# Signs of an adjacency matrix taken in SBUF, and turned by transposing DMAs in place of TensorE

## The chip, the cores and the metric

The kernel runs on one core of a Trainium2 chip. The core has five engines with a queue of instructions each, worked off in order: PE (TensorE, matrix products; its weight loads are shown apart as PEld), DVE (VectorE), ACT (ScalarE), POOL (GpSimd) and SP (SyncE, which here does nothing but issue DMAs). They meet through semaphores. The metric is the device time of one execution in microseconds, the median of several runs; lower is better.

## The reference

It is one layer of a graph network on 16 batches of 1024 nodes with 64 channels. Each node drops some neighbours by their rank in its row of the adjacency matrix, takes three quantiles per channel over what is left, and puts the sum through two small dense layers:

```python
neigh = (adj_ > 0) & ~eye
ni = neigh.astype(jnp.int32)
rank = jnp.cumsum(ni, axis=-1) - ni
nb = ni.sum(-1)
skip = jnp.where(nb > T, (nb + K - 1) // K, 1)          # T, K = 10, 2
skip = jnp.maximum(skip, 1)
sk = skip[:, :, None]
rem = neigh & (sk > 1) & (rank % sk == sk - 1) & mask[:, :, None]
rem = rem | jnp.swapaxes(rem, 1, 2)
adj_d = jnp.where(rem, 0.0, adj_)
nd = adj_d > 0
vals = jnp.where(nd[..., None], x[:, None, :, :], jnp.inf)
s = jnp.sort(vals, axis=2)
...
agg = agg + jnp.asarray(w, x.dtype) * (v_lo + frac * (v_hi - v_lo))   # tau 0.25, 0.5, 0.75
...
out = (1.0 + EPS_GIN) * x + agg
h = jax.nn.relu(out @ W1 + b1)
y = h @ W2 + b2
```

Ahead of it stands a layer norm with a relu (`h`), behind it a residual. The adjacency is symmetric, holds ones and zeros in float32, has ones on the diagonal, and a node has about nine neighbours.

## The kernel before

All of it is `list_layer`; the function `dense_layer` behind a flag doesn't run on this data. A batch goes through a line of generators:

- `load(b)` (L1007): for each of eight tiles of 128 rows, `ask` (L892) has SP fetch 512 KB of adjacency into a buffer `at` (three of them). PE turns it: the upper two bytes of each float are taken as bfloat16 (a view with a step of two), and eight products with the identity (L1021) write two PSUM tiles `tp` of 128x512. A ninth product (L1027) adds a large negative number on the diagonal. Two ACT instructions (L1034) take the sign, once per PSUM tile, into the 8-bit tensor `ne`, which holds the turned matrix as [128, 8, 1024]. There are two buffers `ne`. Batch 0 has every second sign taken by DVE.
- `number(b)` counts the neighbours of each node from `ne` (products `cp`, ACT's `cnt`, L1063).
- `drop(b)` ranks them (products `rk`, ACT's `dist`, L1106, two per row tile) and marks those to drop (`rem`, DVE).
- `keep(b)` combines both directions (products `kp`, ACT's `kept`, L1130) and packs bits (`pack<-code`, L1138).
- `order(b)` and `collect(b)` sort the nodes by degree and write lists of neighbours, `idx`: from `pack<-num` (L1147) through products `codeP` (L1201) and their evacuations `st` and `own` (L1214 to L1219) to the last `idx` (L1253). `choose(b)` fetches the first eight slots of the tile with most neighbours by products (`got`).

The lists then feed gathers: one indirect DMA (L1408) per slot, issued by POOL, brings 128 rows of 64 floats into tiles `g`. The gathers of a pair of batches are sorted along the slots by DVE with minimum and maximum (L1551, L1556), weighted by ACT (L1571), summed by PE (`acc`, L1577) and put through the dense layers. While one pair is sorted, the next one is prepared.

What sets the order on each engine is `arrange`: it gives every instruction a cost (`Step.cost`), schedules the whole program forward and backward some rounds, and fixes each engine's sequence by its best round. The order is thus static; a DMA that lands later than its cost says keeps an engine waiting at that place. Which instruction waits for which data stays with the framework's semaphores. Two buffers' rules matter here: `at` has three buffers, so tile t+3 isn't fetched before tile t is read, and `ne` has two, so batch b+1 isn't written before `keep(b-1)` has read its own.

Of the kernel before, what the change touches and what calls it, by code (L numbers as in the profile page):

```python
# [40 lines left out]
OP = mybir.AluOpType  # L41
# [27 lines left out]
EARLY, AHEAD = 8, 20  # L69
FINAL = (8,4,4,4,0,0,0,0)  # L70
MANY = 10

FEW = 32
GROUP = 8
# [540 lines left out]
class Step:  # L615

    def __init__(self, ins, place):
        self.ins, self.place, self.kind = ins, place, type(ins).__name__
        self.engine = NAMES[str(ins.engine).split(".")[-1]]
        self.reads, self.writes = (  # L620
            [Use(a.bass_ap) for a in aps if getattr(a, "bass_ap", None) is not None] for aps in (ins.ins, ins.outs)
        )
        self.moves = self.kind == "InstDMACopy"
        self.before, self.behind, self.after, self.tail = set(), set(), [], []
        self.busy, self.lag = self.cost()
        self.load = self.lag - 1900

    def cost(self):
# [26 lines left out]
        if self.engine == "POOL":  # L655
            return (1345, 1400) if self.moves else (300 if most <= 128 else 4100, 100)
        by = self.writes[0].size * self.writes[0].count * (self.writes[0].lines[1] - self.writes[0].lines[0])
        return 480, 1900 + by / 390


def spread(steps, waits, ranks, place):
# [169 lines left out]
def list_layer(  # L831
# [106 lines left out]
    nc.vector.tensor_copy(mask.rearrange("p b t -> p (b t)"), mp)  # L938
    below = cst.tile([P, P], BF16, name="below")
    nc.vector.tensor_scalar(below, minus16, MOST, None, OP.mult)  # L940
    near = cst.tile([P, 1], F32, name="near")
    nc.vector.memset(near, -LEAST_EDGE)
    parts = cst.tile([P, NT, P], BF16, name="parts")
# [62 lines left out]

    def load(b, fast=False):  # L1007

        ne = wk.tile([P, NT, N], FP8, name="ne", bufs=2)
        neT[b] = ne  # L1010
        nbs[b] = [wk.tile([P, NT], F32, name=n) for n in ("bias", "half")]
        for t in range(NT):
            ask(b, t)
            at = asked.pop((b, t)).bitcast(BF16).rearrange("p (n two) -> p n two", two=2)[:, :, 1]
            ask(*divmod(b * NT + t + 2, NT))
            for n in range(2):
                tp = psum.tile([P, 4, P], F32, name="tp", tag="mx" if b else "agg", bufs=3 if b else 2)
                run = []
                for s in range(4):
                    m = 4 * n + s  # L1020
                    run.append(nc.tensor.matmul(  # L1021
                        tp[:, s], at[:, m * P:(m + 1) * P], ident16, start=(s == 0), stop=(s == 3 and t // 4 != n),
                        skip_group_check=True,
                    ))
                if t // 4 == n:
                    run.append(
                        nc.tensor.matmul(tp[:, t % 4], below, ident16, start=False, stop=True, skip_group_check=True)  # L1027
                    )
                settle(run)
                to = ne[:, 4 * n:4 * n + 4, t * P:(t + 1) * P]  # L1030
                if not b and n:
                    nc.vector.tensor_scalar(to, tp, 0.0, 0.5, OP.is_gt, OP.subtract, saturate=False)
                else:
                    nc.scalar.activation(to, tp, AF.Sign, bias=near, scale=UP, saturate=False)  # L1034
            if fast and t % 4 == 3:
                number(b, t - 3, t + 1)
            yield 0.1
        if not fast:
            number(b, 0, NT)
        yield 1.4  # L1040

    def number(b, lo, hi):
# [4 lines left out]
        for at in range(lo, hi, step):  # L1047
            cols = slice(at * P, (at + step) * P)

            cp = psum.tile([P, step * P], F32, name="cp", tag="mx", bufs=3)  # L1050
            run = []
            for k in range(2):
                for q in range(4):
                    ones = one if b or q < 2 else twice[:, P:]
                    run.append(nc.tensor.matmul(
                        cp[32 * q:32 * q + 32], ones[:, 1 - k:33 - k], ne[:, 2 * q + k, cols], start=(k == 0),
                        stop=(k == 1), skip_group_check=True,
                    ))
            settle(run)
            if b == 0 and at >= 4:  # L1060
                nc.vector.tensor_scalar(cnt[:, cols], cp, float(P), None, OP.add)
            else:
                nc.scalar.activation(cnt[:, cols], cp, AF.Copy, bias=float(P))  # L1063
# [16 lines left out]
    def drop(b):  # L1080
# [5 lines left out]
        for t in range(NT):  # L1086
            ts = slice(t * P, (t + 1) * P)
            dist = wk.tile([P, N], F16, name="dist")
            for n in range(2):
# [4 lines left out]
                )]  # L1094
                for s in range(4):
                    run.append(nc.tensor.matmul(  # L1096
                        rk[:, s * P:(s + 1) * P], ne[:, 4 * n + s, ts], twice[:, :P] if not b and n else upper,
                        start=False, stop=(s == 3),
                        skip_group_check=True,
                    ))  # L1100
# [9 lines left out]
    def keep(b):  # L1110

        ne, rem = neT.pop(b), rems.pop(b)
        for t in range(NT):
            ts = slice(t * P, (t + 1) * P)
            kept = wk.tile([P, NT, P], FP8, name="kept")
            for n in range(2):
                kp = psum.tile([P, 4, P], F32, name="kp", tag="mx" if b or n else "agg", bufs=3 if b or n else 2)
                side = bool(b <= 3 and n or not b and t % 2)
                run = [] if side else [nc.tensor.matmul(kp, plus, ne[:, 4 * n:4 * n + 4, ts], start=True, stop=False)]
                run.append(nc.tensor.matmul(kp, minus, rem[:, 4 * n:4 * n + 4, ts], start=side, stop=False))  # L1120
                for s in range(4):
                    at = (4 * n + s) * P
# [1 line left out]
                settle(run)  # L1124
                if side:
                    nc.vector.scalar_tensor_tensor(
                        kept[:, 4 * n:4 * n + 4], kp, -1.0, ne[:, 4 * n:4 * n + 4, ts], OP.mult, OP.is_lt, saturate=False
                    )
                else:
                    nc.scalar.activation(kept[:, 4 * n:4 * n + 4], kp, AF.Relu, saturate=False)  # L1130
# [1066 lines left out]
```

## Time and profile before

| | us |
|---|---|
| median of 3 runs | 1337.45 |
| lowest, highest | 1331.23, 1339.11 |
| the profiled execution, its time | 1339.05 |
| the profiled execution, its span (first to last instruction) | 1337.2 |
| mean granted TensorE clock in it | 0.938 |
| DMA: mean rate over the span | 95 GB/s |

The profile is of one execution. "Busy" is the time in which an engine executes something; register, branch, semaphore and DMA-issuing instructions don't count, so SP has no busy time. A group of instructions is a line of the kernel with its engine, operation and shapes: the sum of busy time, the mean of one, then the idle time just before them and what ended it. In a row of windows each engine has its busy time and, in brackets, its number of instructions; PEclk is the granted clock and DMA the mean share of the 16 DMA engines. In the timeline each row has its start, its length, the engine, and in square brackets the idle time before it with the event that came last before the start.

### The profile page before, as it was taken

The numbers are of one execution on the slowest core, as the hardware profiler recorded it, in microseconds if no ns is written. First come the engines' busy times: TensorE is split into PE (matmuls) and PEld (weight loads), VectorE is DVE, ScalarE is ACT, GpSimd is POOL, SyncE is SP. The second block draws the span as 40 slices with busy tenths as digits, with TensorE's granted clock in tenths as the row PEclk, the third lists the DMA queues.
The fourth block names the chain that finished last, engine by engine and source line by source line (L and its number), as shares of the span: only waits on it lengthen the run. The fifth ranks groups of instructions, "written<-read, shape, count | busy, mean of one in ns | idle before, by whom it ended". The sixth has DMA issues, their size and how long they took to land.

```text
span 1337.2 us, 32000 instructions
## 1 busy us (share of the span) xinstructions
PE 1133.7 (85%) x9889; PEld 758.7 (57%) x9931; DVE 1154.8 (86%) x5327; ACT 1101.0 (82%) x3470; POOL 949.3 (71%) x895
## 2 busy tenths in 40 slices
PE   6877789797899998988898899888999999777267
PEld 4555566666556665656565665656566557553144
DVE  6828998859998699965699999999699999999984
ACT  5685899797989997899759995899969998389564
POOL 0177677777777777777777777777777777777740
PEclk9888999998989998999999999999999999787679
DMA  6272526252526251535335252724343122111111
GB/s 230 63 246 54 152 57 171 63 154 55 147 41 187 56 171 33 145 99 146 68 79 151 47 153 56 186 48 131 76 105 90 31 53 60 30 32 42 22 30 29
DMA packets 158739, 126.59 MB, mean 95 GB/s; under 512 B 127163, under 2 KB 127710, under 8 KB 158558
## 3 DMA queue, kind: packets, MB, share of 16 engines
q1 hardware_dynamic: 130078, 95.25, 24.8%
q0 software_dynamic: 28480, 29.20, 11.3%
q8 instruction: 80, 1.31, 0.4%
q14 instruction: 101, 0.83, 0.2%
HBM read 105.62 MB, written 9.05 MB: 86 GB/s over the span
## 4 chain that ended last, share of the span: by engine, by line
ACT 34%; PE 27%; DVE 18%; issue 16%; DMA 4%; POOL 0%; SPq 0%; DVEq 0%; POOLq 0%; ACTq 0%
ACT g L1571 7%; ACT dist L1106 7%; ACT ne L1034 6%; PE codeP L1201 4%; ACT kept L1130 4%; DVE g L1551 4%; DVE g L1556 4%; PE got L1451 3%; PE acc L1577 3%; PE high L1708 2%; DMA g<-gtab,idx 2%; PE kp L1123 1%; DVE keys L1210 1%; DVE found L1241 1%; PE kp L1120 1%
## 5 line engine op out<-in xcount | busy, mean ns | idle before, releaser
L1408 POOL DMA_INDIRECT g<-gtab,idx x856 | 909.7, 1063 | 330.4 <-DMA g<-gtab,idx 132.6
L1551 DVE TENSOR_TENSOR g<-g 128x768 f32<-128x768 f32 (+5 forms) x479 | 290.7, 617 | 15.1 <-PE acc L1631 10.7
L1556 DVE TENSOR_TENSOR g<-g 128x768 f32<-128x768 f32 (+5 forms) x479 | 290.0, 618 | 11.9 <-DMA gg<-g 11.7
L1571 ACT ACTIVATE g<-g,coef 128x64 f32<-128x64 f32 x896 | 254.1, 393 | 36.0 <-DVE g L1551 25.6
L1034 ACT ACTIVATE ne<-tp,near 128x512 fp8e4<-128x512 f32 x248 | 167.7, 763 | 21.8 <-PE tp L1027 12.9
L1577 PE MATMUL acc<-g,kf 128*128 128x128 f32 (+4 forms) x528 | 138.6, 387 | 51.6 <-ACT g L1571 49.9
L1201 PE MATMUL codeP<-pack,perm 128*128 128x332 bf16 x1024 | 171.5, 314 | 6.2 <-DVE perm L1176 6.1
L1106 ACT ACTIVATE dist<-rk,bias 128x512 f16<-128x512 f32 x256 | 170.6, 755 | 4.6 <-PE rk L1096 2.6
L1130 ACT ACTIVATE kept<-kp 128x512 fp8e4<-128x512 f32 x220 | 142.0, 682 | 2.1 <-PE code L1133 1.5
L1201 PEld LDWEIGHTS <-perm 128*128 128x128 bf16 x1024 | 95.6, 100 | 74.3 <-DVE perm L1176 20.6
L1577 PEld LDWEIGHTS acc<-g,kf 128*128 128x128 f32 x528 | 82.5, 200 | 78.4 <-ACT g L1571 68.2
L1021 PE MATMUL tp<-kb,at 128*128 128x128 bf16 x976 | 98.5, 224 | 32.9 <-ACT dist L1106 15.3
L1096 PEld LDWEIGHTS <-ne 128*128 128x128 fp8e4 x1024 | 80.8, 99 | 59.6 <-issue 25.1
L877 DVE MEMSET pause<- 128x1 bf16 x1838 | 108.4, 59 | 0.0
L1096 PE MATMUL rk<-kw,ne 128*128 128x128 fp8e5 x992 | 102.4, 223 | 1.9 <-issue 1.1
L1021 PEld LDWEIGHTS <-at 128*128 128x128 bf16 x976 | 73.2, 101 | 54.0 <-issue 29.1
L1123 PE MATMUL kp<-kw,rem 128*128 128x128 fp8e5 x1024 | 102.0, 218 | 0.0
L1091 PE MATMUL rk<-parts,cnt 128*128 128x512 bf16 x232 | 89.4, 385 | 12.4 <-ACT dist L1106 5.3
L1120 PE MATMUL kp<-rem,kw 128*128 128x512 bf16 x256 | 96.6, 378 | 0.3 <-DVE pause L877 0.3
L1451 PE MATMUL got<-pack,hot 128*128 128x192 bf16 x896 | 96.3, 252 | 0.5 <-DVE y L1762 0.4
L1123 PEld LDWEIGHTS <-rem 128*128 128x128 bf16 x1024 | 73.6, 97 | 38.8 <-issue 0.4
L1107 DVE TENSOR_SCALAR rem<-dist,half 128x1024 bf16<-128x1024 f16 x128 | 63.7, 504 | 24.6 <-ACT dist L1106 20.8
(221 smaller groups left out, 2409.0 us busy)
## 6 DMA issues: line engine op xcount, KB each, us to landing
at<-in_adj_dram SPq DMA_DIRECT2D x122, 512.0 KB
g<-gtab,idx POOLq DMA_INDIRECT x856
xt<-in_x_dram SPq DMA_DIRECT2D x16, 256.0 KB
y<-in_x_dram SPq DMA_DIRECT2D x16, 256.0 KB
gtab<-xt SPq DMA_DIRECT2D x16, 256.0 KB
out_dram<-y SPq DMA_DIRECT2D x14, 256.0 KB
spare<-in_adj_dram SPq DMA_DIRECT2D x6, 512.0 KB
g<-stage SPq DMA_DIRECT2D x14, 160.0 KB
```

The costliest lines, as they stand in the source:

```text
L1021: run.append(nc.tensor.matmul(tp[:, s], at[:, m * P:(m + 1) * P], ident16, start=(s == 0), stop=(s == 3 and t // 4 != n), skip_group_check ...
L1034: nc.scalar.activation(to, tp, AF.Sign, bias=near, scale=UP, saturate=False)
L1096: run.append(nc.tensor.matmul(rk[:, s * P:(s + 1) * P], ne[:, 4 * n + s, ts], twice[:, :P] if not b and n else upper, start=False, stop=(s ...
L1106: nc.scalar.activation(to, rk, AF.Abs, bias=bias[:, t:t + 1])
L1123: run.append(nc.tensor.matmul(kp[:, s], rem[:, t, at:at + P], minus, start=False, stop=(s == 3)))
L1130: nc.scalar.activation(kept[:, 4 * n:4 * n + 4], kp, AF.Relu, saturate=False)
L1201: run.append(nc.tensor.matmul(flat, perm[:, t, k * P:(k + 1) * P], pack[:, t], start=False, stop=(t == NT - 1), skip_group_check=True,))
L1408: ins = nc.gpsimd.indirect_dma_start(out=gathered[m, tiles][:, slot, k - lo, h], out_offset=None, in_=tables[2 * m + h][0], in_offset=bass ...
L1551: nc.vector.tensor_tensor(at(f + k * df, df, many), pa, pb, OP.min if what == "<" else OP.max)
L1556: nc.vector.tensor_tensor(pa if back else pb, pa, pb, OP.max if what == "<" else OP.min)
L1571: nc.scalar.activation(v[:, i, j], v[:, i, j], AF.Copy, scale=w[:, i, j:j + 1])
L1577: nc.tensor.matmul(acc, ident32, lines[:, s], start=False, stop=(s == now[-1] and not ends), skip_group_check=True)
```

## The change

For batches 1 to 15 (`TURN = 1`) PE no longer turns the adjacency. One ACT instruction takes the sign of the whole 128x1024 tile in SBUF and writes it as 8-bit numbers into the first 1024 bytes of each row of the same buffer, so that columns n and n + 512 lie side by side. SP then issues a DMA with a transpose that takes such a pair as one 16-bit number and writes [128, 4, 128] of them into `ne`, so `ne` is now four blocks of pairs, and its readers take it with a step of two bytes. The diagonal, which the ninth product put right, is set by one DVE minimum per batch with `away` (-1 on the diagonal, 1 elsewhere) over the eight diagonal blocks. Batch 0 is turned by PE as before, into the new layout. The planner counts the transposing DMA as a move and gives it a rate of its own.

```diff
+TURN = 1
...
-        self.moves = self.kind == "InstDMACopy"
+        self.moves = self.kind in ("InstDMACopy", "InstDmaTransposeAnt")
...
-        return 480, 1900 + by / 390
+        return 480, 1900 + by / (180 if self.kind == "InstDmaTransposeAnt" else 390)
...
+    away = cst.tile([P, P], BF16, name="away")
+    nc.vector.tensor_scalar(away, minus16, 2.0, 1.0, OP.mult, OP.add)
...
-        ne = wk.tile([P, NT, N], FP8, name="ne", bufs=2)
+        pairs_of = wk.tile([P, NT // 2, N], BF16, name="ne", bufs=2)
+        ne = pairs_of.bitcast(FP8).rearrange("p m (n e) -> p m n e", e=2)
...
-            at = asked.pop((b, t)).bitcast(BF16).rearrange("p (n two) -> p n two", two=2)[:, :, 1]
+            whole = asked.pop((b, t))
+            at = whole.bitcast(BF16).rearrange("p (n two) -> p n two", two=2)[:, :, 1]
             ask(*divmod(b * NT + t + 2, NT))
+            if b >= TURN:
+                nc.scalar.activation(
+                    whole.bitcast(FP8)[:, :N].rearrange("p (n e) -> p e n", e=2),
+                    whole.rearrange("p (e n) -> p e n", e=2), AF.Sign, bias=near, scale=UP, saturate=False,
+                )
+                nc.sync.dma_start(
+                    out=pairs_of[:, :, t * P:(t + 1) * P], in_=whole.bitcast(BF16)[:, :HALF], transpose=True
+                )
+                yield 0.1
+                continue
...
-                to = ne[:, 4 * n:4 * n + 4, t * P:(t + 1) * P]
+                to = ne[:, :, t * P:(t + 1) * P, n]
...
+        if b >= TURN:
+            spot = bass.AP(ne.tensor, ne.offset, [ne.ap[0], [2 * N // 2 + 1, 2], [2 * N + 2 * P, 4], [2, P]])
+            nc.vector.tensor_tensor(spot, spot, away[:, None, None, :].to_broadcast([P, 2, 4, P]), OP.min, saturate=False)
         if not fast:
             number(b, 0, NT)
...
-                        rk[:, s * P:(s + 1) * P], ne[:, 4 * n + s, ts], twice[:, :P] if not b and n else upper,
+                        rk[:, s * P:(s + 1) * P], ne[:, s, ts, n], twice[:, :P] if not b and n else upper,
...
-                run = [] if side else [nc.tensor.matmul(kp, plus, ne[:, 4 * n:4 * n + 4, ts], start=True, stop=False)]
+                run = [] if side else [nc.tensor.matmul(kp, plus, ne[:, :, ts, n], start=True, stop=False)]
...
```

Since `arrange` orders the program anew, instructions move on every engine. Three places show it. Line numbers of the changed kernel are its own: L1022 is the new sign, L1026 the transposing DMA, L1055 the diagonal, L1124 `dist`, L1148 `kept`, L1156 `pack<-code`, L1165 `pack<-num`.

The first place is on ACT, in `keep(0)` up to the start of `order(0)`, on the way to the first lists. Before:

```order
L1138 CAST pack<-code 128x136
L1304 ACTIVATE waste,mean<-xt 128x64
L1307 ACTIVATE mean<-mean 128x8
L1309 ACTIVATE waste,var<-xt,mean 128x64
L1138 CAST pack<-code 128x136
L1309 ACTIVATE waste,var<-xt,mean 128x64 x2
L1138 CAST pack<-code 128x136
L1309 ACTIVATE waste,var<-xt,mean 128x64 x2
L1147 CAST pack<-num 128x8
```

And in the changed kernel:

```order
L1156 CAST pack<-code 128x136
L1322 ACTIVATE waste,mean<-xt 128x64
L1022 ACTIVATE at<-at,near 128x2x512
L1156 CAST pack<-code 128x136
L1325 ACTIVATE mean<-mean 128x8
L1022 ACTIVATE at<-at,near 128x2x512
L1165 CAST pack<-num 128x8
```

The fourth and fifth sign of batch 1 now stand ahead of `pack<-num` of batch 0; three others stand some rows further ahead, and none stood here before.

The second place is on ACT as well, in `drop(1)`. Before, from the first `dist` of batch 1:

```order
L1106 ACTIVATE dist<-rk,bias 128x512 x2
L1034 ACTIVATE ne<-tp,near 128x4x128 x2
L1106 ACTIVATE dist<-rk,bias 128x512 x2
L1034 ACTIVATE ne<-tp,near 128x4x128 x2
L1106 ACTIVATE dist<-rk,bias 128x512 x2
L1034 ACTIVATE ne<-tp,near 128x4x128 x2
```

And in the changed kernel, the whole of `drop(1)` with what stands ahead of it:

```order
L1081 ACTIVATE cnt<-cp 128x512 x2
L1364 CAST pack<-mask 128x8
L1666 COPY g_1060<-g_1052 32x64 x2
L1022 ACTIVATE at<-at,near 128x2x512
L1475 CAST stage<-got 128x128
L1476 CAST stage<-got 128x128x2
L1022 ACTIVATE at<-at,near 128x2x512
L1475 CAST stage<-got 128x128
```

```order
L1022 ACTIVATE at<-at,near 128x2x512
L1124 ACTIVATE dist<-rk,bias 128x512 x7
L1022 ACTIVATE at<-at,near 128x2x512
L1124 ACTIVATE dist<-rk,bias 128x512 x9
```

Before, every pair of `dist` was followed by a pair of signs of the next batch. Now the sixteen `dist` stand nearly alone, and the signs are spread over what comes ahead of them and behind.

The third place is on SP, with the fetches of batches 1 and 2. Before, around the first fetches of batch 2:

```order
L892 DMA at<-in_adj_dram 128x1024
L1275 DMA gapart<-apart 16x13 x2
L892 DMA at<-in_adj_dram 128x1024 x5
L1400 DMA g_1050<-stage 128x3x64
L892 DMA at<-in_adj_dram 128x1024 x2
```

And in the changed kernel, from the first transposing DMA on:

```order
L1026 DMA_TRANSPOSE ne<-at 128x4x128 x3
L893 DMA at<-in_adj_dram 128x1024 x3
L1026 DMA_TRANSPOSE ne<-at 128x4x128 x3
L893 DMA at<-in_adj_dram 128x1024 x3
L1411 DMA g_1052<-own 128x64
L1026 DMA_TRANSPOSE ne<-at 128x4x128 x3
L893 DMA at<-in_adj_dram 128x1024
```

A fetch into a buffer now stands behind the transposing DMA that reads it, and the queue's other DMAs stand behind both; before, a fetch waited for PE's products.

More of the change, by code (lines that the diff above doesn't have):

```diff
@@ L1055, in number @@
                     run.append(nc.tensor.matmul(
-                        cp[32 * q:32 * q + 32], ones[:, 1 - k:33 - k], ne[:, 2 * q + k, cols], start=(k == 0),
+                        cp[32 * q:32 * q + 32], ones[:, 1 - k:33 - k], ne[:, (2 * q + k) % 4, cols, q // 2], start=(k == 0),
                         stop=(k == 1), skip_group_check=True,
@@ L1126, in keep @@
                     nc.vector.scalar_tensor_tensor(
-                        kept[:, 4 * n:4 * n + 4], kp, -1.0, ne[:, 4 * n:4 * n + 4, ts], OP.mult, OP.is_lt, saturate=False
+                        kept[:, 4 * n:4 * n + 4], kp, -1.0, ne[:, :, ts, n], OP.mult, OP.is_lt, saturate=False
                     )
```

## The prediction

> **What bounds the kernel now.** I read the page's table of engines first, then its chain of waits.
>
> ```profile
> PE 1133.7 (85%) x9889; PEld 758.7 (57%) x9931; DVE 1154.8 (86%) x5327; ACT 1101.0 (82%) x3470; POOL 949.3 (71%) x895
> ACT 34%; PE 27%; DVE 18%; issue 16%; DMA 4%; POOL 0%; SPq 0%; DVEq 0%; POOLq 0%; ACTq 0%
> ```
>
> Taken alone, this says that PE, ACT and DVE share the span, and that POOL is idle for 29% of it and never on the chain. The table by stages tells another story:
>
> ```profile
> core 0: us, PE busy (x) PEld busy (x) DVE busy (x) ACT busy (x) POOL busy (x), PEclk, DMA share, GB/s
> 80.00:100.00 20.00, 14.98 (x160) 10.06 (x160) 4.97 (x25) 19.52 (x34) 15.38 (x16) 1.00 0.84 258
> 120.00:140.00 20.00, 12.60 (x69) 7.52 (x69) 17.88 (x102) 4.81 (x28) 8.98 (x9) 0.84 0.21 39
> 210.00:228.00 18.00, 16.15 (x177) 10.82 (x175) 16.90 (x92) 18.00 (x34) 13.55 (x14) 1.00 0.86 237
> 660.00:680.00 20.00, 18.33 (x120) 10.93 (x122) 19.30 (x100) 7.88 (x33) 15.13 (x17) 1.00 0.23 45
> 1260.00:1280.00 20.00, 4.89 (x19) 4.29 (x20) 20.00 (x74) 6.22 (x25) 16.04 (x14) 0.50 0.11 23
> 60.00:700.00 640.00, 558.02 (x5269) 383.14 (x5290) 524.63 (x2468) 549.17 (x1749) 484.49 (x465) 0.96 0.43 112
> 700.00:1280.00 580.00, 488.49 (x3978) 319.60 (x3991) 555.25 (x2565) 487.48 (x1511) 452.28 (x415) 0.92 0.32 77
> ```
>
> ACT swings between 4.8 and 20 us of 20, POOL stands at 15 to 16 in all rows but one. Why it is not at 20 is in POOL's timeline and its waits:
>
> ```profile
> start us, us, engine line op out<-in xcount [idle before <-releaser]
> 55.98 1.10 POOL L1408 DMA_INDIRECT g<-gtab,idx  x1 [54.09 <-DVE ones_r L979]
> ...
> 62.98 1.32 POOL L1408 DMA_INDIRECT g<-gtab,idx  x1 [3.38 <-ACT ne L1034]
> ...
> 130.48 0.95 POOL L1408 DMA_INDIRECT g<-gtab,idx  x1 [0.30 <-DMA g<-gtab,idx]
> 140.52 1.15 POOL L1408 DMA_INDIRECT g<-gtab,idx  x1 [9.10 <-ACT index_h L1428]
> 141.98 1.10 POOL L1408 DMA_INDIRECT g<-gtab,idx  x1 [0.30 <-ACT rows L1439]
> ...
> 1284.47 0.94 POOL L1408 DMA_INDIRECT g<-gtab,idx  x1 [0.30 <-DMA g<-gtab,idx]
> ```
>
> ```profile
> POOL g L1408 <- DMA g<-gtab,idx: 132.6, 433, 0.9
> ```
>
> A gap of 0.30 us stands before a gather whatever released it, so it belongs to each gather and is no wait. With it, POOL is full: from 700 to 1280 us it has 452.3 + 415 x 0.305 = 578.9 of 580 us; from 60 to 700, 484.5 + 465 x 0.305 = 626.3 of 640. The missing 13.7 us are mostly 9.10 - 0.30 = 8.8 us at 131, when the lists of batch 1 weren't written yet, and 3.1 us at 60. So from 56 us to the last gather at 1285.4 us POOL issues one gather after the other, and 51.8 us follow behind (sort and dense layers of the last tiles). The chain misses it because it takes each 0.30 us for a wait and leaves POOL there for the engine named. The floor with these gathers is 1337.2 - 13.7 = 1323.5 us, unless the first starts earlier, one takes less, or the tail shrinks. DVE is the second bound: 555 of 580 us in the second half.
>
> **The change, part by part.** The rows that price it:
>
> ```profile
> L1408 POOL DMA_INDIRECT g<-gtab,idx x856 | 909.7, 1063 | 330.4 <-DMA g<-gtab,idx 132.6 <-DVE ones_r L979 54.1 <-DVE pause L877 16.5
> L1034 ACT ACTIVATE ne<-tp,near 128x512 fp8e4<-128x512 f32 x248 | 167.7, 763 | 21.8 <-PE tp L1027 12.9 <-PE tp L1021 8.7
> L1021 PE MATMUL tp<-kb,at 128*128 128x128 bf16 x976 | 98.5, 224 | 32.9 <-ACT dist L1106 15.3 <-DMA at<-in_adj_dram 12.6 <-ACT ne L1034 1.0
> L1027 PE MATMUL tp<-kb,below 128*128 128x128 bf16 x128 | 29.2, 228 | 0.0
> L1551 DVE TENSOR_TENSOR g<-g 128x768 f32<-128x768 f32 x112 | 106.1, 948 | 10.8 <-PE acc L1631 10.7
> L1343 ACT CAST pack<-xt x16: 1051/1144/1271, 31.9 to 1071.0; 128x1024 bf16<-128x1024 uint8 x16
> L892 SPq DMA_DIRECT2D at<-in_adj_dram x122: 323/328/789, 1.3 to 1006.4; - x122
> 915.52 3.57 DMA at<-in_adj_dram
> ```
>
> *PE, removed.* 960 products at 98.5/976 = 0.101 us and 120 on the diagonal at 0.228: 124 us of PE's 1133.7. Hidden: POOL is full all the while, so this by itself is worth nothing at the end.
>
> *ACT.* 240 signs at 167.7/248 = 0.676 us, 162 us, become 120 of 1024 columns from SBUF. The nearest row is L1343, as wide and in SBUF: 1.05 to 1.27 us, I take 1.144, so 137 us. ACT gets back 25 us (10 to 36), hidden as well. What counts is where they stand: from 210 to 228 us ACT was full (18.00 of 18.00) with `dist` and signs in turn, 16 each; now `drop` needs half of that.
>
> *POOL's stall at 131.* The chain's rows date batch 1:
>
> ```profile
> 61.06 1.74 ACT ne L1034 x3
> ...
> 81.58 1.31 ACT dist L1106 x2
> ...
> 98.57 1.16 ACT dist L1106 x2
> ```
>
> It was signed from 61 us on and dropped from 81 to 99. Now its last two signs stand between the first and second evacuation of `codeP` in `collect(0)`, ahead of 60 us, and its `drop` is nearly bare of signs, so its lists come about 15 to 20 us earlier, and the stall of 8.8 us goes: **-8.8**. What is late next is nothing that POOL showed: no other gap is above 0.9 us.
>
> *The way to the first gather.* Signs 4 and 5 now stand ahead of `pack<-num`, which leads to the first lists:
>
> ```profile
> 34.52 0.60 ACT L1130 ACTIVATE kept<-kp 128x512 fp8e4<-128x512 f32 x1 [1.45 <-PE code L1133]
> 42.78 0.23 ACT L1147 CAST pack<-num 128x8 bf16<-128x8 f32 x1
> ```
>
> Signs 1 and 2 fill the idle 1.45 us at 33. The first one's buffer then goes through sign 1.14, issue 0.5, transpose T, fetch 3.57, so sign 4 starts at 33 + 5.2 + T and sign 5 is done 2.3 us behind it: at 40.5 + T against 42.78. With T = 3 that is **+1**.
>
> *T itself.* No row shows a transposing DMA. Nearest are plain transfers: the 512 KB fetch took 3.57 us, so 128 KB moved at that pace and with its fixed part lie between 0.9 and 3.57. From above, the page's queue row:
>
> ```profile
> q1 hardware_dynamic: 130078, 95.25, 24.8%
> ```
>
> That is 0.248 x 1337.2 x 16 / 130078 = 41 ns per packet. If the crossbar cut the 128 KB as finely as 32 bytes, 4096 packets over 16 engines took 10.5 us. I take 3 us, near the plain transfer, and keep 0.9 and 10.5 for the range. On SP each costs between 0.32 and 0.79 us to issue; I take 0.5, 60 us in all on a queue with 357 other rows. Behind a transposing DMA that waits for its sign stand the next fetch, `g<-own` and `gtab<-xt`, which fetch ahead of need.
>
> The Trainium skill, "VectorE: DVE Perf Modes", The three transpose paths, speaks against the change: 1309 ns for a 128x128 block by the crossbar, 390 ns by TensorE, and TensorE wherever PSUM will do. Four blocks make 5.2 us, an estimate, by which the term above would be +3 in place of +1. Its "Advanced Engine Details and Errata", X-Bar Transpose (TRN2), says that transposing DMAs are as fast as regular ones, by which it would be about 0. No run here shows either yet.
>
> *Per batch.* A buffer's round is 5.2 + T = 8.2 us, eight tiles over three buffers need 22 us, and a batch comes every 67 us (14 of them from the signs at 61 to the last fetch at 1006 us). So the transposes have room, the more as signs stand well ahead of `number`.
>
> *DVE, added.* 15 minima over 128x1024. Nearest is the minimum over 768 columns, 0.948 us; scaled, 1.26. It can't be under 0.948 by much: 15 to 19 us, I take 1.25 each. The first stands in `collect(0)`, ahead of the indices for the fourth gather, which already waited 3.1 us: **+1.2**. Five fall behind 700 us, 6.2 us, where DVE has 25 us left: I count half, **+3**. The others lie beside idle DVE.
>
> *The readers' step of two bytes.*
>
> ```profile
> L1021 PEld LDWEIGHTS <-at 128*128 128x128 bf16 x976 | 73.2, 101 | 54.0 <-issue 29.1 <-DMA at<-in_adj_dram 17.5
> L1096 PEld LDWEIGHTS <-ne 128*128 128x128 fp8e4 x1024 | 80.8, 99 | 59.6 <-issue 25.1
> L1119 PE MATMUL kp<-ne,kw 128*128 128x512 fp8e4 x220 | 83.2, 378 | 0.8 <-ACT kept L1130 0.6
> ```
>
> Weights with a step of two (`at`) load in 101 ns, those without (`ne`) in 99: nothing. A moving operand with a step isn't shown; its ends are nothing and twice the 83.2 us of L1119. I take nothing, and PE's 124 us would cover the other end.
>
> Sum: -8.8 + 1 + 1.2 + 3 = -3.6 on the span of 1337.2, so 1333.6. The profiled run took 1339.05, 1.6 above the median of 1337.45; the same -3.6 from the median gives 1334.
>
> **The rivals.**
>
> *Faster: the chain of waits is right.* Then PE's 124 us and ACT's 18 us stages are the pace. `drop` shrinks from 18 to 9 us in 14 batches, 126 us, and the signs go back elsewhere at 9.2 us a batch, partly into idle ACT (91 us from 60 to 700). With 3.5 us a batch left, 1337 - 50 = 1287; a weaker form, in which only all of POOL's gaps go and the tail tightens, ends near 1318. For it: the chain, and DVE's idle 115 us from 60 to 700. Against it: POOL's 578.9 of 580.
>
> *Slower: T is long.* ACT's order is fixed, so each late fetch holds ACT, and behind it the evacuations of `codeP`. Two rounds a batch wait, 30 in all, each for T - 3. ACT has 91 + 93 us idle between 60 and 1280, of which I let 130 absorb. It decides at T = 3 + 130/30 = 7.3 us; at 10.5 the excess is 95 us, plus 7.5 at the first gather: up to 1430. In the middle, T = 8.5, 1337 + 35 + 5 - 9 = 1368. Against it: the plain rows.
>
> *Slower: DVE becomes the bound.* If a minimum waits at the head of DVE's queue for the last transpose, 2 us fifteen times beside 19 us of work, the second half gives +16 on top: 1350.
>
> **How the numbers follow.** A measurement of this kernel can tell about 1% from no change, 13.4 us: below 1324 is faster, above 1351 slower. The likeliest, POOL's pace kept, has 0.46 and its own range is 1324 to 1346. The chain as the pace has 0.24 (most of it the weak form, around 1318), a long T 0.20, DVE as the bound 0.10, of which half is over 1351, as are 0.03 of the likeliest with a late first gather. So faster 0.24, same 0.48, slower 0.28. The range for 8 in 10 reaches from 1310 (the weak form of the faster rival inside, the strong one out) to 1368 (the middle of long T).
>
> **What would show it.** Right: POOL's gap at 131 us gone, its other gaps still 0.30, `drop` stages of about 10 us, PE busy near 1010 us, 51 to 52 us behind the last gather, and a first gather between 56 and 59 us. T shows in the time from a transposing DMA's issue to the fetch that waits for it. Wrong: gaps of POOL above 1 us after 150 (lists late: T), ACT waiting for `at`, DVE waiting at the minimum, or gathers of another mean length than 1.063 us, which my floor takes as given.

## The result, and the profile after

The changed kernel takes 1379.97 us (median of 4 runs, 1372.86 to 1388.49), the kernel before beside it 1335.76. The ratio is 1.033 (1.0295 to 1.0365): slower, 12 us above the forecast range. The profiled run took 1388.49 us, its span is 1386.7, its granted clock 0.880 (before: 0.938).

The page's engines and its chain of waits, as shown of before:

```profile
PE 1094.0 (79%) x8851; PEld 713.6 (51%) x8851; DVE 1175.4 (85%) x5343; ACT 1089.9 (79%) x3350; POOL 957.9 (69%) x895
PE 30%; ACT 20%; DVE 18%; issue 18%; DMA 10%; SPq 2%; POOL 1%; DVEq 0%; POOLq 0%; ACTq 0%
```

No engine got busier by 50 us: DVE has 20.6 us more, with the minima, POOL 8.6 more, PE and ACT have less. In the chain DMA's share grew most (4% to 10%) and ACT's fell (34% to 20%). So the time is in waits, and POOL's timeline says where:

```profile
start us, us, engine line op out<-in xcount [idle before <-releaser]
56.06 1.10 POOL L1426 DMA_INDIRECT g<-gtab,idx  x1 [54.17 <-DVE mean L1332]
...
140.42 1.25 POOL L1426 DMA_INDIRECT g<-gtab,idx  x1 [5.08 <-ACT idx L1275]
...
256.40 0.94 POOL L1426 DMA_INDIRECT g<-gtab,idx  x1 [20.00 <-DMA at<-in_adj_dram]
...
1335.88 0.94 POOL L1426 DMA_INDIRECT g<-gtab,idx  x1 [0.30 <-DMA g<-gtab,idx]
```

The gathers start where they did (56.06, before 55.98), and the last ends at 1336.8 in place of 1285.4. That is 51.4 us later; with a tail 1.9 us shorter it makes the 49.5 us by which the span grew. Two things make up the 51.4, in these groups (busy time and mean, then the idle time before):

```profile
L1426 POOL DMA_INDIRECT g<-gtab,idx x856 | 919.4, 1074 | 370.3 <-DMA g<-gtab,idx 138.5 <-DVE mean L1332 54.5 <-DMA at<-in_adj_dram 20.8
L1022 ACT ACTIVATE at<-at,near 128x1024 fp8e4<-128x1024 f32 x120 | 138.8, 1164 | 75.0 <-DMA at<-in_adj_dram 57.5 <-issue 15.3 <-ACT index_h L1446 0.8
```

The gathers' sum grew by 9.7 us. The other 41.6 are time of POOL beyond gathers and their 0.30 us, nearly all of it waits. And ACT now stands idle 75.0 us ahead of signs, mostly for a fetched tile; before it was 21.8. SP's waits tell why the tile is late:

```profile
SPq L1026 <- PE code L1151: 95.6, 9, 17.4
SPq L893 <- DMA ne<-at: 59.1, 46, 3.9
SPq L1026 <- DMA at<-in_adj_dram: 24.9, 17, 2.6
```

46 of the fetches wait for a transposing DMA to leave their buffer, 59.1 us in all. The DMA itself waits nine times, up to 17.4 us, for `keep` of two batches earlier to leave `ne` (first row; the product named there is the last event ahead of it). That second wait isn't the loss by itself: e10 below, which loses nothing, still has 54.5 us of it, five times and up to 19.1. The timeline of the changed kernel ahead of the 20 us shows one such case:

```profile
231.87 3.86 SPq L1026 DMA_TRANSPOSE ne<-at  x3
236.21 1.50 SPq L893 DMA_DIRECT2D at<-in_adj_dram  x3
240.34 2.43 ACT L1022 ACTIVATE at<-at,near 128x1024 fp8e4<-128x1024 f32 x2 [1.55 <-DMA at<-in_adj_dram]
241.52 1.21 SPq L1026 DMA_TRANSPOSE ne<-at  x1
...
244.37 2.55 SPq L1026 DMA_TRANSPOSE ne<-at  x2
246.97 0.57 SPq L893 DMA_DIRECT2D at<-in_adj_dram  x1
...
250.74 1.15 ACT L1022 ACTIVATE at<-at,near 128x1024 fp8e4<-128x1024 f32 x1 [1.67 <-issue]
...
251.84 0.23 ACT L1236 CAST own<-codeP 128x64 bf16<-128x64 f32 x1
...
255.31 0.26 DVE L1271 SCALAR_TENSOR_TENSOR idx<-bit,low 128x104 int32<-128x104 f32 x1
```

Three signed tiles hold all three buffers `at` until `ne` is free at 231.87. Then each step follows the one ahead: three transposing DMAs of 1.2 us on SP, the fetches, the next signs at 240.34, again DMAs, fetch, sign at 250.74. Behind that sign, in ACT's fixed order, stands an evacuation of `codeP`, from it come the last candidates, from them `idx` at 255.31, and with it the gather at 256.40.

The new instructions themselves, in the view of one line (min, median, max in ns):

```profile
L1026 SPq DMA_TRANSPOSE ne<-at x120: 1188/1220/2597, 31.6 to 998.4; - x120
```

From the start of its issue to the release of what waited, the chain of waits has five of them:

```profile
68.76 6.37 DMA ne<-at
86.53 4.39 DMA ne<-at
133.45 4.20 DMA ne<-at
172.40 3.42 DMA ne<-at
654.34 3.86 DMA ne<-at
```

### The profile page after: what moved, and what is told of

The parts are those of the page before. It is cut to its first block, busy times and chain, and to the rows that moved or that the text cites. A ratio compares the mean times of both kernels' runs of the same rounds, so it can differ in the third digit from the quotient of the medians.

```text
span 1386.7 us, 30087 instructions
## 1 busy us (share of the span) xinstructions
PE 1094.0 (79%) x8851; PEld 713.6 (51%) x8851; DVE 1175.4 (85%) x5343; ACT 1089.9 (79%) x3350; POOL 957.9 (69%) x895
## 4 chain that ended last, share of the span: by engine, by line
PE 30%; ACT 20%; DVE 18%; issue 18%; DMA 10%; SPq 2%; POOL 1%; DVEq 0%; POOLq 0%; ACTq 0%
DMA at<-in_adj_dram 6%; PE codeP L1219 4%; DVE g L1574 4%; ACT dist L1124 4%; PE got L1469 4%; DVE g L1569 4%; ACT kept L1148 3%; ACT g L1589 3%; PE acc L1595 2%; PE high L1726 2%; ACT at L1022 2%; PE rk L1109 2%; PE yp L1776 2%; DMA ne<-at 2%; PE hp L1759 2%
## 5 line engine op out<-in xcount | busy, mean ns | idle before, releaser
L1426 POOL DMA_INDIRECT g<-gtab,idx x856 | 919.4, 1074 | 370.3 <-DMA g<-gtab,idx 138.5
L1569 DVE TENSOR_TENSOR g<-g 128x512 f32<-128x512 f32 (+5 forms) x479 | 290.4, 619 | 5.0 <-DMA g<-stage 3.9
L1574 DVE TENSOR_TENSOR g<-g 128x256 f32<-128x256 f32 (+4 forms) x479 | 290.6, 619 | 2.2 <-DMA gg<-g 1.2
L1595 PE MATMUL acc<-g,kf 128*128 128x128 f32 (+4 forms) x528 | 155.0, 430 | 76.3 <-ACT g L1589 72.7
L1219 PE MATMUL codeP<-pack,perm 128*128 128x332 bf16 x1024 | 188.2, 335 | 12.4 <-DVE perm L1194 11.1
L1022 ACT ACTIVATE at<-at,near 128x1024 fp8e4<-128x1024 f32 x120 | 138.8, 1164 | 75.0 <-DMA at<-in_adj_dram 57.5
L1124 ACT ACTIVATE dist<-rk,bias 128x512 f16<-128x512 f32 x256 | 157.2, 706 | 15.1 <-DVE hot L1461 10.5
L1595 PEld LDWEIGHTS acc<-g,kf 128*128 128x128 f32 x528 | 94.9, 224 | 114.5 <-ACT g L1589 102.9
L1148 ACT ACTIVATE kept<-kp 128x512 fp8e4<-128x512 f32 x220 | 139.8, 671 | 2.0 <-ACT pack L1156 0.5
L1109 PE MATMUL rk<-parts,cnt 128*128 128x512 bf16 x256 | 103.5, 404 | 17.3 <-ACT dist L1124 14.8
L1137 PE MATMUL kp<-ne,kw 128*128 128x512 fp8e4 x220 | 83.2, 378 | 0.7 <-ACT kept L1148 0.3
L1469 PEld LDWEIGHTS <-hot 128*128 128x128 bf16 x896 | 75.8, 100 | 9.3 <-DVE hot L1461 3.4
```

Of the source, the lines that this page charges most:

```text
L1022: nc.scalar.activation(whole.bitcast(FP8)[:, :N].rearrange("p (n e) -> p e n", e=2), whole.rearrange("p (e n) -> p e n", e=2), AF.Sign, bi ...
L1124: nc.scalar.activation(to, rk, AF.Abs, bias=bias[:, t:t + 1])
L1219: run.append(nc.tensor.matmul(flat, perm[:, t, k * P:(k + 1) * P], pack[:, t], start=False, stop=(t == NT - 1), skip_group_check=True,))
L1426: ins = nc.gpsimd.indirect_dma_start(out=gathered[m, tiles][:, slot, k - lo, h], out_offset=None, in_=tables[2 * m + h][0], in_offset=bass ...
L1469: nc.tensor.matmul(got[:, q], hot[:, j, at + q], pack[:, j, VALUES:], start=(j == 0 and q == 0), stop=(j == NT - 1 and q == 1), skip_group ...
L1569: nc.vector.tensor_tensor(at(f + k * df, df, many), pa, pb, OP.min if what == "<" else OP.max)
```

## The experiments

The theories that the expectations name. A: the buffer's round (fetch, sign, transposing DMA, next fetch) is late, ACT and then POOL wait; A1, because the order was planned with wrong costs; A2, because the round is too long in any order. B: the pair layout or a new order costs by itself. C: one accident at 236 us. D: contention with the gathers. E: the minima, the long sign or DVE. F: a minimum lengthens the gathers that meet it; G: it doesn't. H: any new order lengthens the gathers.

**e1 to e4, under other conditions.** Edits: `TURN = 16`; `TURN = 8`; the sign straight into `ne`; the planner's cost (the last two stand at e8 and e7).

> All 16 batches are turned by PE into the new pair layout; no transposing DMA, no minimum, all readers with their step of two bytes. Theory A (the buffer's round: fetch, sign, transposing DMA of 1.22 us on SP where the order was planned with 0.48, and only then the next fetch; ACT stands 75.0 us at signs, the lists come late, POOL waits): without transposing DMAs the time is that of the kernel before, 1336 within 7, POOL's only wait above 4 us after 100 us is the 9 us at 131, gathers 1.06 us. Rival B (the pair layout with its step, or the program's being ordered anew, costs by itself): above 1355.

> PE turns batches 0 to 7, the transposing DMAs batches 8 to 15 (64 in place of 120). Theory A: the loss follows the waits of POOL that lie where batches 8 to 15 are loaded (523 to 998 us: 3.25, some of 0.4 to 3.2 between 589 and 681, 1.8, 4.3, 1.5, about 20 us in all), so 1356 (1345 to 1365), and no wait of 20 us at 236 us. Rival C (single accident: only the 20 us at 236 and what follows from it): the time of the kernel before, 1336 to 1342. Rival D (contention: each transposing DMA slows the gathers beside it): half of the gathers' 8.6 us, with POOL's gaps staying 0.30.

> Leaves out the turning of batches 1 to 15: the sign of a tile's 128 rows goes straight from the fetched tile into ne, as block t of the pair layout (this adjacency is symmetric, so the numbers in ne are the same). Sign count, forms of ACT's and DVE's instructions, the minimum and the layout stay as in the changed kernel; PE's 124 us are gone as there. Theory A: the loss is in the transposing DMAs alone, so this ends at POOL's pace, 1325 (1315 to 1340), with ACT's idle time ahead of signs under 25 us. Rival E (the minima, the one long sign in place of two short ones, or DVE): 1355 to 1380, as before the transposes were taken out.

> Order only: the planner counts 1.25 us on SP for a transposing DMA and 4.3 us until it has landed, near the trace's 1.22 and 3.4 to 6.4, in place of 0.48 and 2.6. Theory A1 (the order is wrong because its costs are): signs are planned where their fetches have landed, ACT's 75 us ahead of signs fall below 35, POOL's waits below 25 us, time 1340 to 1355. Theory A2 (the round itself is too long, whatever the order): signs can't be placed better, ACT or the lists are late all the same, 1370 to 1385.

The kernel before took 1706.73 us here (12 runs), and the four 1.024, 0.999, 0.967 and 0.992 of it. In e1's list of waits, idle time of POOL ahead of gathers for which the profile names no event makes 256.6 us:

```profile
POOL g L1426 <- issue: 256.6, 438, 16.5
```

Instructions are about as long as elsewhere (a gather 1043 ns on average), the gaps are longer; where they come from isn't known. Such gaps cover waits of a few us, so nothing is concluded from these four. Three were run again; the half dose (e2) was not, and C is answered by e17.

**e5, the changed kernel again**, no edit.

> The changed kernel itself, with the kernel before beside it. In the four runs so far the kernel before took 1707 us and engines stood idle with no cause that the profile names, so they can only be read against the changed kernel under the same conditions. If the kernel before takes about 1336 us here, the ratio is 1.033 again (1.027 to 1.039). If it takes 1707 again, every theory has the changed kernel near the true-cost order's 0.992 (0.98 to 1.01), because idle time of other origin then covers waits of a few us.

1.032 (1.028 to 1.036), with the kernel before at 1335.68, as in all runs from here on within 2 us. ACT's idle time ahead of signs is 65.8 us, POOL's longest wait again one at 234 us, of 17.4.

**e6, signs in buffers of their own.**

```diff
-                    whole.bitcast(FP8)[:, :N].rearrange("p (n e) -> p e n", e=2),
+                    signs.bitcast(FP8).rearrange("p (n e) -> p e n", e=2),
...
-                    out=..., in_=whole.bitcast(BF16)[:, :HALF], transpose=True
+                    out=..., in_=signs, transpose=True
...
-        stage = wk.tile([P, EARLY, C], F32, name="stage", bufs=2)
+        stage = wk.tile([P, EARLY, C], F32, name="stage", bufs=1)
```

> The sign is written to a buffer of its own (1 KB per partition, two of them, room for which comes from the second buffer stage), so a fetch waits for the sign alone and no longer for the transposing DMA to land; a transposing DMA still takes 1.22 us on SP, and the planner still counts 0.48. Theory A2 (the round of the buffer is what is late): the 46 waits of a fetch for a transposing DMA (59.1 us) go, ACT's 75 us ahead of signs fall below 30, ratio 1.00 to 1.015. Theory A1 (the order, planned with wrong costs, holds ACT at places where the data isn't there): waits shift from fetches to the transposing DMAs, ratio 1.02 to 1.04. One buffer stage in place of two may cost up to 5 us by itself.

1.025 (1.021 to 1.029). There are two buffers `signs` of 1 KB per partition, and one `stage` less. The group of signs:

```profile
L1023 ACT ACTIVATE signs<-at,near 128x1024 fp8e4<-128x1024 f32 x120 | 138.1, 1160 | 46.8 <-DMA ne<-signs 44.2 <-issue 1.3 <-ACT own L1238 0.6
```

ACT no longer waits for fetches but, 44.2 us, for the transposing DMA to leave `signs`. The wait moved, as A1 had it: freeing the fetch alone leaves most of the loss.

**e7, the true costs.** Only the planner's numbers change, 1.25 us on SP and 4.3 us behind it (5.5 from the issue's start, inside the 3.4 to 6.4 of the chain).

```diff
-        return 480, 1900 + by / (180 if self.kind == "InstDmaTransposeAnt" else 390)
+        return (1250, 4300) if self.kind == "InstDmaTransposeAnt" else (480, 1900 + by / 390)
```

> As e4 (the planner counts 1.25 us on SP and 4.3 us to the landing of a transposing DMA; nothing else changes), where the kernel before takes about 1336. Theory A1 (what is late is late because the order was planned with wrong costs): ACT's idle time ahead of signs falls from 64 to 75 us to below 35, POOL's longest wait after 100 us from 17 to 20 us to below 6, ratio 1.000 to 1.012. Theory A2 (the round is too long whatever the order): ratio 1.02 to 1.035, and the idle time stays.

1.009 (1.005 to 1.013), A1's range, and ACT waits 7.6 us in place of 75.0:

```profile
L1022 ACT ACTIVATE at<-at,near 128x1024 fp8e4<-128x1024 f32 x120 | 139.5, 1173 | 7.6 <-DMA at<-in_adj_dram 6.8 <-ACT dist L1124 0.5
```

The same instructions in another order: 2.3 of the 3.2% were the order's. But POOL's longest wait didn't fall below 6 us, it moved to the lists of batch 1:

```profile
149.93 0.94 POOL L1426 DMA_INDIRECT g<-gtab,idx  x1 [16.82 <-ACT index_h L1446]
```

**e8, no turning.**

```diff
-                    whole.bitcast(FP8)[:, :N].rearrange("p (n e) -> p e n", e=2),
-                    whole.rearrange("p (e n) -> p e n", e=2), AF.Sign, ...
-                nc.sync.dma_start(out=..., in_=..., transpose=True)
+                    ne[:, t % 4, :, t // 4], whole, AF.Sign, ...
```

> As e3: leaves out the turning of batches 1 to 15 (the sign goes from the fetched tile straight into ne, as block t of the pair layout; this adjacency is symmetric). Theory A: 0.985 to 1.000 of the kernel before, gathers back to 1.06 us, PE's saving of 124 us still without effect because POOL is the pace. Rival E (minima on DVE, the one long sign, or the order made anew): 1.02 to 1.035, as with the transposing DMAs.

1.008 (1.005 to 1.011): neither A's 0.985 to 1.000 nor E's 1.02. The transposing DMAs are gone, ACT waits 9.1 us at signs, and the gathers' sum is still 919.1 us. Sums of other orders differ by more than D's 8.6 us (table below), so this alone doesn't refute D. But in the changed kernel's timeline, up to 1010 us, the 281 gathers that overlap the 5.5 us from the start of a transposing DMA's issue last 1.050 us on average, the 361 others 1.080. So D falls.

**e9, PE turns into the pair layout.** `TURN = 16`.

> As e1: PE turns all 16 batches into the pair layout, no transposing DMA and no minimum. Theory A: 0.995 to 1.008 of the kernel before. Rival B (the layout's step of two bytes in what PE reads and ACT writes): 1.015 or more, with the products that read ne (kp, cp, rk) or the signs longer than before. In e1 the ratio was 1.024 where the kernel before took 1707 us; if that was the layout, it shows here too.

1.011 (1.005 to 1.018), above A's range and below B's. The products that read `ne` are as before (`kp` 379 ns, `rk` 222); POOL's waits are 7.9 us shorter than before, and the gathers 18.0 us longer:

```profile
L1426 POOL DMA_INDIRECT g<-gtab,idx x856 | 927.7, 1084 | 324.0 <-DMA g<-gtab,idx 140.3 <-DVE ones_r L982 51.9 <-DVE pause L878 13.1
```

**e10, both: signs apart and true costs.**

> e6 and e7 together: signs in buffers of their own (one buffer stage in place of two), and true costs for the transposing DMA. Theory A1 with A2 (both matter): better than either alone, 0.99 to 1.005. If only the costs matter: as e7 within 0.004. If only the buffers matter: as e6, 1.025.

1.0006 (0.9985 to 1.0026): the loss is gone, which neither part alone did.

```profile
L1023 ACT ACTIVATE signs<-at,near 128x1024 fp8e4<-128x1024 f32 x120 | 140.0, 1172 | 4.3 <-DMA ne<-signs 4.1
```

**e11 and e12, one true cost each.** `(1250, 1900 + by / 180)` and `(480, 4300)` for the transposing DMA.

> As e7, but only the planner's time on SP for a transposing DMA is mended (1.25 us in place of 0.48); its landing stays planned at 0.73 us of wire and 1.9 us behind. If SP's issue was the term that mattered: as e7, 1.005 to 1.013 of the kernel before. If the landing was: 1.02 to 1.033.

> As e7, but only the planned landing is mended (2.4 us of wire and 1.9 us behind, 4.3 in all, near the trace's 3.4 to 6.4); SP's time stays planned at 0.48 us. If the landing was the term that mattered: 1.005 to 1.013. If SP's issue was: 1.02 to 1.033. Both between, 1.013 to 1.02: each carries a part.

1.017 (1.013 to 1.021) and 1.012 (1.007 to 1.016); ACT waits 43.6 and 11.9 us ahead of signs:

```profile
L1022 ACT ACTIVATE at<-at,near 128x1024 fp8e4<-128x1024 f32 x120 | 139.1, 1168 | 43.6 <-DMA at<-in_adj_dram 40.1 <-issue 2.1 <-ACT g L1589 0.7
```

```profile
L1022 ACT ACTIVATE at<-at,near 128x1024 fp8e4<-128x1024 f32 x120 | 139.7, 1177 | 11.9 <-DMA at<-in_adj_dram 10.3 <-DMA gg<-g 1.3 <-ACT apart L1282 0.2
```

Each takes a part of the loss; the landing takes more of ACT's waits. Their intervals overlap at 1.013 to 1.016, so which matters more for the time isn't settled.

**e13 and e14, the minimum twice and the minimum replaced**, both on e10: the instruction written twice, and two instructions that set a bit in 512 pairs each (0.41 us apiece, 0.82 for 1.22).

```diff
-            nc.vector.tensor_tensor(spot, spot, away[:, None, None, :].to_broadcast([P, 2, 4, P]), OP.min, saturate=False)
+                nc.vector.tensor_tensor(spot, spot, away[:, e, None, :].to_broadcast([P, 4, P]), OP.bitwise_or)
```

> e10 with the diagonal's minimum issued twice in a row (the second changes nothing): 15 more DVE instructions of 1.22 us. Theory F (a gather that meets a minimum on DVE lasts until about 0.8 us behind the minimum's end, as in rows of 1.9 us beside 0.94, so the 15 minima lengthen the gathers by some 8 us in all): the gathers' sum grows by 5 to 11 us more (mean 1.074 to about 1.083), ratio 1.004 to 1.010. Rival G (gathers are longer for another reason, the minimum only takes DVE's time): gathers stay at 1.074 within 0.004, ratio 0.998 to 1.004.

> e10 with the diagonal set in 16-bit pairs: two DVE instructions that set a bit of 512 pairs each in place of one minimum over 1024 single bytes. If 16-bit operands go at twice the pace on DVE, 0.3 us each and 0.65 us in all in place of 1.22. Theory F: fewer and shorter meetings, gathers 3 to 6 us shorter than in e10, ratio 0.993 to 1.000. Rival G: gathers as in e10, ratio 0.998 to 1.003.

1.005 (1.003 to 1.007) and 1.004 (1.002 to 1.006). The gathers' sums are 920.7 and 922.7 us beside e10's 919.7: neither 5 to 11 more nor 3 to 6 less. But each of these is a new order too, and the sum mixes both. The single gathers in the timelines tell more. In e10, 14 gathers start during a minimum and last 1.48 us on average, those that meet none 1.065. In e13 it is 31 with 1.37 beside 1.064, in e14 five with 1.09 beside 1.078. By these means the minima lengthen the gathers by about 6 us in e10, 9 in e13 and next to nothing in e14. In the changed kernel it is 13 gathers with 1.48 beside 1.068, about 5 of the 9.7 us. So F's meeting is there, somewhat below the 8 us it was given. What it does to the sum over a run is covered by the order, and in the time no price of it shows.

**e15 to e18, a new order alone.** The planner's margin between engines, `LATE`, is 60 or 40 ns in place of 50: the kernel before twice, the changed one, and e10.

> The kernel before, ordered anew: the planner's margin between two engines (LATE) is 60 ns in place of 50; no instruction is added or taken away. Theory H (a new order by itself lengthens the gathers, since they meet other DVE instructions, and this is the rest of 0.8 to 1.1% in e8 and e9): gathers' sum 913 to 928 us in place of 910, ratio 1.004 to 1.012. Rival (the rest belongs to the pair layout or the minimum): ratio 0.996 to 1.003.

> As e15 with a margin of 40 ns. The same ranges; the two together show how far an order made anew moves the time of the kernel before.

> The changed kernel with its wrong costs, ordered anew with a margin of 60 ns. If the loss comes from the wrong costs: ratio still 1.02 to 1.04, and ACT's idle time ahead of signs 50 us or more. If the order of the changed kernel was merely an unlucky one: 1.00 to 1.015.

> e10 (signs apart, true costs) ordered anew with a margin of 60 ns. With e10's 1.0006 it shows whether transposing DMAs with room and true costs cost anything beside the order: 0.995 to 1.005 if not, above 1.008 if e10 was a lucky order. Below 0.995 it would beat the kernel before.

| | ratio | interval | span | first gather | gathers' sum | waits and rest | tail | ACT idle at signs |
|---|---|---|---|---|---|---|---|---|
| before | | | 1337.2 | 56.0 | 909.7 | 58.9 | 51.8 | 21.8 |
| changed | 1.033 | 1.030 to 1.037 | 1386.7 | 56.1 | 919.4 | 100.5 | 49.9 | 75.0 |
| e7 true costs | 1.009 | 1.005 to 1.013 | 1347.8 | 54.7 | 920.7 | 68.9 | 42.6 | 7.6 |
| e8 no turning | 1.008 | 1.005 to 1.011 | 1338.3 | 58.3 | 919.1 | 63.8 | 36.3 | 9.1 |
| e9 turned by PE | 1.011 | 1.005 to 1.018 | 1345.1 | 53.8 | 927.7 | 51.0 | 51.8 | 19.1 |
| e10 apart, true costs | 1.001 | 0.999 to 1.003 | 1337.0 | 55.7 | 919.7 | 64.9 | 36.0 | 4.3 |
| e15 before, 60 | 1.001 | 1.000 to 1.003 | 1330.7 | 55.4 | 924.4 | 55.2 | 35.1 | 16.7 |
| e16 before, 40 | 1.004 | 1.002 to 1.005 | 1335.5 | 54.3 | 913.6 | 51.9 | 54.9 | 18.0 |
| e17 changed, 60 | 1.037 | 1.035 to 1.040 | 1372.4 | 59.5 | 912.0 | 87.2 | 52.9 | 51.6 |
| e18 apart, 60 | 1.004 | 1.002 to 1.006 | 1339.7 | 57.5 | 930.6 | 57.8 | 33.1 | 5.1 |

Each row is a profiled run in us: start of the first gather, sum of the 856, what POOL had between first and last besides (less 855 gaps of 0.305 us, 260.8; some 36 us of it are the 26 gathers of `gg` in all kernels), and what follows the last. These four columns and the 260.8 add up to the span.

The changed kernel is slow in a second order too (1.037), with a longest wait of 8.9 us at 233 in place of 20: C falls, the loss comes with the wrong costs and not from one accident. The kernel before, merely reordered, has gathers of 913.6 and 924.4 us and 1.001 and 1.004: H is right about the gathers (9.7 us of e15's are one gather at the end) and wrong about the time: in e15 the tail is 16.7 us shorter, in e16 the waits are 7.0 us shorter. e18 lies within its 0.995 to 1.005, so e10 was no lucky order.

No kernel here beats the kernel before. e10 equals it.

## Why the prediction was wrong

- **The pace.** Borne out, though not by the table's sums, which add up by construction: e8, e10 and e18 lack PE's turning as well, ACT waits 4 to 9 us at signs there, POOL's waits and rest are 58 to 65 us beside 58.9 before, and none of them is faster. PE's saved products were worth nothing at the end.
- **The stall at 131, -8.8.** The gap is 5.08 us now, but it ends where it did, at 140.42 (before 140.52). It is shorter because the gathers ahead of it end at 135.34 in place of 131.43; 2.6 us of that are longer gathers. So nothing of the 8.8 was gained. The changed kernel's `drop(1)` is bare of signs, as said,

```profile
80.61 2.46 ACT L1124 ACTIVATE dist<-rk,bias 128x512 f16<-128x512 f32 x4
...
86.41 5.30 ACT L1124 ACTIVATE dist<-rk,bias 128x512 f16<-128x512 f32 x9
```

and done at 91.7 in place of 99.7. But it starts at 80.6, where it did before (81.6), not 15 to 20 us earlier: the tiles of batch 1 came late. And what `drop` gained was lost on the way to the lists:

```profile
131.82 1.15 ACT L1022 ACTIVATE at<-at,near 128x1024 fp8e4<-128x1024 f32 x1 [4.45 <-issue]
...
137.68 1.23 DVE L1055 TENSOR_TENSOR ne<-ne,away 128x1024 fp8e4<-128x1024 fp8e4 x1 [5.66 <-DMA ne<-at]
...
139.34 0.26 DVE L1271 SCALAR_TENSOR_TENSOR idx<-bit,low 128x104 int32<-128x104 f32 x1
```

ACT stands idle ahead of a sign, DVE stands 5.66 us at a minimum for a transposing DMA (the one at 133.45 in the chain above), and the last `idx` of batch 1 stands behind that minimum. In e5 the gap is 0.7 us and ends at 138.04.
- **The first gather, +1, and the fourth, +1.2.** 0.1 us later, 1.4 in e5; POOL's wait behind the third is 3.22, before 3.38. No term of weight.
- **SP's issue and T.** 0.5 us, with 0.79 as the bound; measured 1.19 or more on all 120, 1.22 at the median. The changed kernel's hardware queue moves 65280 packets more, 544 each:

```profile
q1 hardware_dynamic: 195358, 110.99, 30.8%
```

T = 3 behind an issue of 0.5 makes 3.5 from its start; the five rows have 3.4 to 6.4, so behind the issue T was 2.2 to 5.2. The Trainium skill, "VectorE: DVE Perf Modes", The three transpose paths, gave an estimate of 5.2 us for T; with 1.2 of issue that is 6.4, and the longest of the five rows has it. Its "Advanced Engine Details and Errata", X-Bar Transpose (TRN2), by which these would be as fast as regular transfers, doesn't fit: a fetch of four times the bytes took 3.57 us in the row of before, though fetches of the changed kernel were slower at times (9.70 us for one at 123.31 in its chain).
- **The step that failed: "So the transposes have room, the more as signs stand well ahead of `number`."** I compared 22 us of rounds with 67 us per batch. On average that holds even with what was measured: 1.16 for the sign, 3.4 to 6.4 and 3.57 for the fetch make a round of 8 to 11 us, so 22 to 30 of 67. But ACT's order is fixed, and the planner set signs among the evacuations of `codeP` by 0.48 us of issue and a landing at 3.1; there every late tile holds the lists. What is late next was not nothing: ACT's idle time ahead of signs rose from 21.8 to 75.0 us, and POOL's waits and rest by 41.6. e7 shows that the costs behind the order did most of this, e11 and e12 that each of the two costs did a part. The 0.9% from e7 to e10 may be the buffer that is freed earlier; since e8 is 0.8% slow without any transposing DMA, it may also be the order.
- **The rival "T is long" had the mechanism and the wrong threshold.** It was to decide at T = 7.3, since 130 us of ACT's idle time were to absorb the excess. It decided below that: with the longer issue counted in, its T was 2.9 to 5.9. Idle time on average doesn't lie where the tiles are late. The prediction's signs of being wrong were all there: POOL's gaps after 150 us, ACT waiting for `at`, DVE waiting at the minimum, and longer gathers.
- **DVE.** A minimum took 1.22 us (1.25 said) and DVE stood idle ahead of it for a transposing DMA five times, 12.2 us, not fifteen; the 5.66 us of one of them held the lists of batch 1. With true costs (e7, e10) it never did. e13 and e14 lie 0.4 and 0.3% above e10, one with more of it and one with less, so no price of its own is shown.
- **The step of two bytes, nothing.** Right: the weights `ne` load in 102 ns (before 99), and `kp` takes 378 as before.
- **PE near 1010 us.** It is 1094.0. The mean granted clock fell from 0.938 to 0.880, and of the products that did not change some got longer (`codeP`), others not (`kp`), here in before and in the changed kernel:

```profile
L1201 PE MATMUL codeP<-pack,perm 128*128 128x332 bf16 x1024 | 171.5, 314 | 6.2 <-DVE perm L1176 6.1
```

```profile
L1219 PE MATMUL codeP<-pack,perm 128*128 128x332 bf16 x1024 | 188.2, 335 | 12.4 <-DVE perm L1194 11.1 <-ACT at L1022 1.1
L1137 PE MATMUL kp<-ne,kw 128*128 128x512 fp8e4 x220 | 83.2, 378 | 0.7 <-ACT kept L1148 0.3
```

- **The gathers at 1.063 us, taken as given.** 1.074, 9.7 us in all. About 5 of these are the gathers that start during a minimum (e13 and e14). From e5 on every other order has 912 to 931 us, with or without transposing DMAs and minima, so the order moves the sum by more than that. The tail of 52 was taken as given too; it lies between 33 and 55.

Open: e8 and e9 are 0.8 and 1.1% slower, more than the 0.1 and 0.4% of a new order alone. Whether that is the layout or two poor orders isn't settled. In e9 seven gathers of over 2 us, six of them between 472 and 558 us, take 20.5 us together and so hold 13 of its 18 us; what holds them up was not tested.

## What to carry to other kernels

Where a planner fixes the order, measure a new instruction's queue time and landing first: here the same instructions cost 3.2 to 3.7% in orders made with guessed costs, 0.9% with measured ones, and 0.1 to 0.4% once the buffer was also freed earlier. Room is to be looked for at the place of the wait (which instruction stands behind it in the queue), not as an average per stage. An operation in place ties its buffer to the slowest reader, here a DMA's landing.

## What the runs showed of the hardware

A gather that starts during a minimum lasts beyond it. In the changed kernel's timeline:

```profile
197.20 0.94 POOL L1426 DMA_INDIRECT g<-gtab,idx  x1 [0.30 <-DMA g<-gtab,idx]
...
198.30 1.23 DVE L1055 TENSOR_TENSOR ne<-ne,away 128x1024 fp8e4<-128x1024 fp8e4 x1 [2.90 <-DMA ne<-at]
...
198.45 1.89 POOL L1426 DMA_INDIRECT g<-gtab,idx  x1 [0.30 <-DMA g<-gtab,idx]
```

The gather ahead of it takes 0.94 us; this one ends at 200.34, 0.81 behind the minimum's end. So do all 13 gathers that start during a minimum there, by 0.81 to 0.92 us. The Trainium skill, "SBUF — State Buffer", SBUF: two separate sides, states that a VectorE instruction with two SBUF inputs and a GpSimd instruction that reads SBUF share a port pair as an exclusive lock, held by whichever starts first for its whole length. The rows agree with that. The gathers' sum over a run goes with the order as well (e13 to e16).

Less work on PE lowered its clock: 0.88 to 0.91 in the kernels from e5 on without PE's turning, 0.93 to 0.94 in those with it (e9, e15, e16, before). Of 124 us of removed products 40 came off PE's busy time. The Trainium skill, "TensorE: Matmul & The Clock Gate", What's actually happening, has the clock depend on how busy PE has just been; the means agree, single windows aren't shown here.
